# Layer 0's weighted sums with the features stationary, two heads on the two column halves of the array, turned back through DRAM

## The chip, the core and the metric

The program runs on one core of one Trainium2 chip. The metric is the device time in microseconds of one execution. Two runs of the kernel before gave 2604.69 and 2605.58 us, with a median of 2605.14 us. TensorE is written PE here, its weight load PEld, VectorE DVE, ScalarE ACT, GpSimd POOL, and the engine whose queue issues the DMAs SP.

## The reference, cut to what matters

The input is 128 graphs of 128 nodes with 256 features, `x` (128, 128, 256), and one adjacency matrix for each graph, `adj` (128, 128, 128), with entries 0 and 1. Four layers follow each other, each with a residual sum and a layer norm: attention with 4 heads of 64 features (layer 0), three steps of a gated recurrent unit (layer 1), a relational sum (layer 2), attention with one head (layer 3). The change is in layer 0:

```python
Wh = (X @ W).reshape(B, N, H, F)                  # H = 4 heads, F = 64 features
e = leaky_relu(e_src[:, :, None, :] + e_dst[:, None, :, :], 0.2)
alpha = softmax(where(A > 0, e, NEG_INF), axis=2)
Hout = einsum('bijh,bjhf->bihf', alpha, Wh)       # the weighted sums
x = layernorm(x + elu(Hout))
```

All data are 32-bit floats.

## The kernel before, in words

The graphs are worked in 33 groups: one of 2, then 31 of 4, then one of 2. A group passes through stages, each written as a generator: `l` loads, `h` layer 0 (`head`), `u` and `v` the elementwise work of the recurrent unit for the two halves of the features (`chunk`), `p` and `q` its matrix products (`gates`, two gates each), `t` layers 2 and 3 (`tail`). The order of all work is written out by hand as strings: each letter advances one stage of one group to its next `yield`. `START` (with the letters of `FIRST`) fills the pipeline, `STEPS` (`PERIOD`) is one period and is run 29 times, `END` (`LAST`) drains it. The instructions of each engine run in exactly the order in which the strings emit them; that holds for the DMAs on SP too. A period advances stages of up to seven groups (offsets 2 to -4).

In `head`, the scores of two graphs (`em`, 128 x 1024: 2 graphs x 4 heads x 128 columns) go through the softmax without its division. A first turn through DRAM follows: `to_dram` writes `em`, `from_dram` reads it back as 32 x 32 squares into `aT` (four DMAs), and DVE transposes within the squares (line 550). Only for group 0 (`by_pe`) does PE turn it. Then each head's `aT` is the stationary operand and that head's 64 columns of `wh` are the moving one: 8 matrix products of 64 columns for two graphs (line 132, called in `head`), into one bank `ps` of PSUM with nodes on the partitions. DVE multiplies the bank by the reciprocal denominators `den` straight into `x1` (line 558). Such a set of 8 products is called a block below; there are 64 of them (two for each group of 4, one for each group of 2), 63 with `by_pe` off.

`em` and `aT` share a ring of three buffers. The banks of PSUM are rings of three (`ps`), three (`sums`) and three (`gate`) by tag. `bank` adds products of zeros (`still`, 512 columns) ahead of the banks that `WARM` lists, 22 of them in the program.

In `gates` a product of two block matrices is done with seven instead of eight partial products, so that partial results have to be moved between halves of two banks: after the first products, ACT copies the half `c21` of `gate` into the half `c11` of `sums` (line 638) and `c22` aside into `p5` (line 640), DVE adds `c12 = c21 + p5` (line 648), and later `c22 = c21 + p5` (line 656). After each of these, PE adds further products into the same banks, so each is a hand-over from PE to another engine and back to PE. In `neighbours`, ACT copies a bank into `agT` (line 611), which PE then takes as a moving operand: another hand-over. The order strings set how much other PE work lies inside each hand-over.

A turn through DRAM in `turn_rows` and `chunk` is the same pair of DMAs with a DVE transpose behind it; SP issues the read only after the write has landed.

Of the kernel before, what the change touches and what calls it, by code (L numbers as in the profile page):

```python
# [9 lines left out]
F32 = mybir.dt.float32  # L10
# [3 lines left out]
ALU = mybir.AluOpType  # L14
AX = mybir.AxisListType

P = 128
N = 128
D = 256
C = D // P  # L20
H, F = 4, 64
# [2 lines left out]
Q = 32  # L24
G = 4
GATES, OTHERS = 3, 2
WARM = {0: 1, 5: 4, 16: 1, 23: 1, 24: 1, 1555: 1, 1557: 5, 1558: 1, 1563: 4, 1568: 3}
BY_PE = {"head": (0,), "rows0": (0, 1, 2), "gru1": (0, 1, -1, -2), "gru2": (0, 1, -1, -2), "rows3": (-1,), "tail": (-1, -2)}
EPS = 1e-5
SLOPE = 0.2  # L30
# [21 lines left out]

FIRST = {"a": ("f", 0), "b": ("c", 0), "c": ("h", 0), "d": ("l", 1), "e": ("h", 1), "f": ("l", 2), "g": ("u", 0), "h": ("q", 0), "i": ("v", 0), "j": ("p", 0), "k": ("h", 2), "l": ("l", 0), "m": ("l", 3), "n": ("u", 1), "o": ("q", 1), "p": ("v", 1), "q": ("p", 1), "r": ("h", 3), "s": ("t", 0)}
START = """
abbbbcccacaccacaccaccccacaccbcacaaaacadcccdcacccaaccbcccccececcceeccebeceecceeceecefccceecefecacccca
cgghegbhiiihehijjhghejaaeieeihhjeejjejjajjadhjehjbjjeijjeajaiakhgghjhjhehijhelajhakgejahhghjeagghaaj
khhgieiggggeheiggihjgejiihgeeeekkiehjliijkjeijeeehiihjkeikhjjhhjkjeeijkjekjhjiejhjkkaikhajkjkjkhgaak
hghhaejhehhhgaikjmheknnghanjogjiognhpaqqqgmpqiopigqqphpoqqqghikrkpqooqgqgniokqoigkoqoaqpkpoqioqoiion  # L60
goqqkpoqggoqqojkikolqqkjoppnniijjpokjhiokjhnnkjhniljojfjhnhojhpjjhjgnrnphhnkjpjinjhipjjiknhkhhjkggjj
hjonhgnkjihrpkkhpkkkkpohkqoqikhrhqgqpkhgqhgqokphqgkroqhpqkrpiqirqkoqirnsqoboqorpkrqqokrqqpqsroopsooq
nqrknorqrqnnorsssooo
"""
PERIOD = {"a": ("t", -3), "b": ("p", -1), "c": ("q", -1), "d": ("t", -2), "e": ("u", -1), "f": ("v", -1), "g": ("h", 0), "h": ("l", 2), "i": ("u", 0), "j": ("q", 0), "k": ("p", 0), "l": ("v", 0), "m": ("h", 1), "n": ("t", -4), "o": ("l", 1), "p": ("l", -1), "q": ("h", 2), "r": ("t", -1)}
STEPS = """
abcdefghdiiccjifkeafdjdkdljckeeicdddfdkmmknloldjkljlkedkfjmkmlejfjknamkfdmmamkfkdjeikjikldkldekkdjed
dlaikjjdjdkbemkdfdkbkjbfnbmjbkajffjjbjfpmblbmbibjjlajcfchbdjccqlimicdcbilddmidbddcqlcimeddmabdbnbccd
fibmlfmaqfbbamlibcceeccmbbdceeclccbcibciddcfcmidfedecidemcjmqfklmjnklfkqqkjmmqmlkjfjmkmllmmkdkkqkjdr
mmdrlmkkjmdqkqmjikqjjqkqrlkdkkkljrjmikljjkjdkrjqiqikijjjqr  # L70
"""
LAST = {"a": ("l", -1), "b": ("t", -4), "c": ("p", -3), "d": ("q", -3), "e": ("h", -2), "f": ("v", -3), "g": ("u", -2), "h": ("t", -5), "i": ("u", -3), "j": ("q", -2), "k": ("v", -2), "l": ("p", -2), "m": ("h", -1), "n": ("t", -6), "o": ("t", -2), "p": ("t", -1), "q": ("l", -3), "r": ("t", -3), "s": ("u", -1), "t": ("v", -1), "u": ("p", -1), "v": ("q", -1), "w": ("l", -2)}
END = """
abcdbefbgghggdiidhjkfbdljbdllbbjikllbkjbmbbjilkmkfklljmfmhniljbimlihhjjnflmlbgllkfjmfbkolblkmimjbmlm
ihfjgllfnjcblcbjbimlcmljmjbjlfjmjbflnggjpchcjfkfjmgcghbcddbcmmjfckkhdcdbjcgcmgiddcgbbbdgdckmdfkmdbob
fcfbcimbcbkdccdbddjcckiiddbmbccdqgkmddkcmmgibmdfmfddiikbgmdljgimdbfflgkljlklfjjbmlbkllkhjljlnrllmljl
mhjjkblkrlkjmlmmjjjlggbjrllrgbjjrjllbjrblrbjlmmkrstjusbjrsrrvugvgjgkvukrsghgrgrrujvkuttrrtuktgtukvuu
rukkrbuvrvubrurgvsgvrusruuukvtuugukuktrtuvsrlvugslrgvsvlkrvsrhvulvtwvlkjlvjjlbvvllvjltjlsvvjklrjjjsg
rtbsrthjlrtrlrhkkrrlrbsbspkljjllrlbrgjbtslsltsbvgjjlgsgrtlvttjljjjtkujurtrkjguvgurbkujtvrvujvuugujku
vtkusuuvououvovtoutruvrovsvvvuruuvvorvvuurvtaosusooouvstrtovvosvotosrsotsrtostrotsvrsvoovuststousovu  # L80
tvbtuvtvvutrouvuuuuovoovotovuuouutrooroootsoourrsouvvuovuuvvvuusovsbuuvstusvvtsvvstttotpopoopoppboro
poooppoppprprpprpopppoppooppoppopppporpppopporppppopoppppppppppppoppopoopppppppppp
"""


# [5 lines left out]
def kernel(ctx: ExitStack, tc: tile.TileContext, a: dict, out: bass.AP):  # L91
    nc = tc.nc
# [4 lines left out]
    NG = len(sizes)  # L97
    spans = [slice(sum(sizes[:i]), sum(sizes[: i + 1])) for i in range(NG)]

    cp = ctx.enter_context(tc.tile_pool(name="const", bufs=1))  # L100
    sp = ctx.enter_context(tc.tile_pool(name="work", bufs=1))
# [6 lines left out]
    def ring(pool, shape, dtype, tag, name, bufs):  # L108

        k = taken[tag] = (taken.get(tag, -1) + 1) % bufs  # L110
        return pool.tile(shape, dtype, tag=f"{tag}_{k}", name=name, bufs=1)
# [4 lines left out]
    def bank(*shape, tag="ps"):  # L116

        t = ring(pp, [P, 512], F32, tag, tag, OTHERS if tag == "ps" else GATES)
        banks["taken"] = banks.get("taken", -1) + 1
        for _ in range(WARM.get(banks["taken"], 0)):  # L120
            nc.tensor.matmul(t, still[:, :P], still, start=True, stop=True)
        n = 1
        for s in shape:
            n *= s
        if len(shape) == 1:
            return t[:, :n]
        names = "abcd"[: len(shape)]
        sizes = {k: s for k, s in zip(names[1:], shape[1:])}
        return t[:, :n].rearrange(f"p ({' '.join(names)}) -> p {' '.join(names)}", **sizes)

    def matmul(ps, lhsT, rhs, start=True, stop=True):
        nc.tensor.matmul(ps, lhsT, rhs, start=start, stop=stop)  # L132
# [10 lines left out]
    nc.gpsimd.memset(negbig, NEG)  # L143

    spread = cp.tile([P, NG], F32, tag="spread", name="spread")

    def squares(t, src):

# [151 lines left out]
    def to_dram(name, *parts):  # L300

        d = ring(dp, [sum(part.shape[1] for part in parts) * P, P], F32, "turn", f"d_{name}", 8)
        lo = 0
        for part in parts:
            hi = lo + part.shape[1] * P
            nc.sync.dma_start(d[lo:hi].rearrange("(k p) m -> p k m", p=P), part)
            lo = hi
        return d

    def from_dram(t, d):  # L310

        squares(t, d)
        return t
# [140 lines left out]
    def head(st):  # L454

        g0, n, by_pe = st["g"], st["n"], st["by_pe"]["head"]
        if by_pe:
            xT = sp.tile([P, C, n * N], F32, tag="x0s", name=f"x0s_{g0}")
            for c in range(C):
                ps = bank(n, N)  # L460
# [3 lines left out]
        else:  # L464
            xT = st["x0s"]
            flat = xT.rearrange("p c m -> p (c m)")
# [9 lines left out]
        for g in range(G):  # L476
            if g < n:
                ps = bank(D + 2 * H)
# [48 lines left out]
        for k in range(0, G, 2):  # L527
# [2 lines left out]
                if not by_pe:  # L530
                    from_dram(aTs[k].rearrange("p g h n -> p (g h n)"), ems[k])
            yield
        y = ring(sp, [P, n, D], F32, "x1", f"x1_{g0}", 3)
        nc.vector.reciprocal(den, den)
        yield
        for k in range(0, G, 2):
            if k >= n:
                for _ in range(3):
                    yield
                continue  # L540
            aT = aTs[k]
            if by_pe:
                for j in range(2):
                    ps = bank(H, N)
                    for h in range(H):
                        transpose(ps[:, h, :], ems[k][:, j, h, :])
                    nc.vector.tensor_copy(aT[:, j], ps)
            else:
                flat = aT.rearrange("p g h n -> p (g h n)")
                nc.vector.transpose(flat, flat)  # L550
            yield
            cols = slice(k * H, (k + 2) * H)
            ps = bank(2, H, F)
            for j in range(2):
                for h in range(H):
                    matmul(ps[:, j, h, :], aT[:, j, h, :], wh[:, k + j, ts(h, F)])
            yield
            nc.vector.tensor_tensor(
                y[:, k : k + 2, :].rearrange("p g (h f) -> p (g h) f", h=H),
                ps.rearrange("p g h f -> p (g h) f"),  # L560
                den[:, cols].unsqueeze(2).to_broadcast([P, 2 * H, F]),
                ALU.mult,
            )
            yield
        yield from residual_elu_norm(y, "x0", st, "x1", "0")
        st["edge"] = ring(sp, [P, n, N], F32, "edge", f"edge_{g0}", 4)
# [169 lines left out]
    def tail(st):  # L736
# [31 lines left out]
        for k in range(0, G, 2):  # L768
            half(k)
            yield  # L770
        adj_T = st["adj_s"]
        step = n // relations

        def related(k):
            rel = sp.tile([P, step, relations, N], F32, tag="rel", name=f"rel_{g0}_{k}")
            rows = adj_T.rearrange("p (g n) -> p g n", g=n)[:, k : k + step, :]
            for r in range(relations):
                nc.vector.tensor_scalar(rel[:, :, r, :], rows, float(r + 1), None, ALU.is_equal)
            return rel
# [1 line left out]
        later = rest()  # L781
        next(later)
        if by_pe:
            nc.vector.transpose(adj_T, adj_T)
            rel = related(0)
        yield
        yield from later
        x2 = st["x2"]
        if not by_pe:
            nc.vector.transpose(adj_T, adj_T)  # L790
            rel = related(0)
        y = ring(sp, [P, n, D], F32, "x3", f"x3_{g0}", 2)
        half, rest = layernorm(y, st, "x3")
# [141 lines left out]
            last[i.engine] = i  # L935


    total = sp.tile([P, 1], F32, tag="total", name="total")
    nc.vector.tensor_reduce(total, spread, AX.X, ALU.add)
    ones = sp.tile([P, 1], F32, tag="ones", name="ones")  # L940
    nc.vector.memset(ones, 1.0)
    ps = bank(1)
# [58 lines left out]
```

## Time and profile before

| | |
|---|---|
| median of 2 runs | 2605.14 us |
| the profiled execution | 2605.27 us |
| its span, first to last instruction | 2603.5 us |
| busy share of the span: PE, PEld, DVE, ACT, POOL | 99%, 87%, 82%, 73%, 32% |
| mean granted PE clock | 0.996 of full |
| DMA | 353.75 MB in 1,495,113 packets, 136 GB/s |
| DMA share of its 16 engines, between 400 and 2300 us | 0.76 to 0.77 |
| blocks of layer 0 (line 132, 128x64) | 1024 records, 273 ns mean |

One 32-bit matrix product appears as two records on PE, one for each of two passes, and as two weight loads on PEld; a transpose by PE has one record of each. A record of a product lasts longer than the distance to the next, since products are pipelined: what a product costs is the distance from its start to the start of the next. In a line of the timeline, the columns are the start in us, the length in us, engine, line, operation, output and input tiles, shape, and the number of instructions merged into the line; in brackets stands the idle time ahead and what ended it. In a line of the table by stretch, the columns are the stretch, its length, the busy time of PE, PEld, DVE, ACT and POOL with the number of instructions, the granted clock, the DMA share and GB/s.

### The profile page before, as it was taken

How to read it: one execution, taken by the hardware profiler on the slowest of the kernel's cores; microseconds unless marked ns; L12 is line 12 of the kernel's file. 1: busy time of each engine (PE TensorE's matmuls, PEld its weight loads, DVE VectorE, ACT ScalarE, POOL GpSimd, SP SyncE). 2: the span in 40 equal slices, each digit the busy share in tenths (PEclk: the TensorE clock that was granted, in tenths of full speed). 3: DMA queues.
4: the chain of work that ended last, by engine and by line, in shares of the span. 5: the costliest groups of instructions: out<-in, count | busy, mean ns of one | idle time of the engine just before them, and what ended most of it. 6: DMA issues, size and time to landing. Idle time of an engine off the chain costs nothing. (4 is left out here: it accounts for less than half of the span.)

```text
span 2603.5 us, 43906 instructions
## 1 busy us (share of the span) xinstructions
PE 2568.5 (99%) x13488; PEld 2263.5 (87%) x13488; DVE 2137.3 (82%) x4570; ACT 1899.3 (73%) x5099; POOL 841.4 (32%) x923
## 2 busy tenths in 40 slices
PE   8999999999999999999999999999999999999997
PEld 5888888888888888888888888888888888888885
DVE  5778888888888888888888888888888888887775
ACT  5666777777777777777777777777777777776666
POOL 0233423333322333323333323333322333332332
PEclk9999999999999999999999999999999999999999
DMA  5456777876777777777787777787778787777431
GB/s 124 75 107 126 139 145 145 151 150 141 148 143 150 148 150 140 151 138 152 146 152 147 140 148 147 148 148 150 139 147 153 145 153 145 140 141 135 92 58 36
DMA packets 1495113, 353.75 MB, mean 136 GB/s; under 512 B 1176280, under 2 KB 1479512, under 8 KB 1494872
## 3 DMA queue, kind: packets, MB, share of 16 engines
q1 hardware_dynamic: 1494872, 350.87, 69.8%
q8 instruction: 111, 1.82, 0.3%
q14 instruction: 130, 1.06, 0.1%
HBM read 213.00 MB, written 137.72 MB: 135 GB/s over the span
## 5 line engine op out<-in xcount | busy, mean ns | idle before, releaser
L628 PE MATMUL gate<-T_a,factors 128*128 128x256 f32 (+1 forms) x2376 | 686.0, 373 | 0.4 <-DVE gate L656 0.4
L628 PE MATMUL gate<-T_h,factors_h 128*128 128x256 f32 (+1 forms) x2376 | 676.1, 375 | 3.6 <-DVE gate L656 3.2
L628 PEld LDWEIGHTS gate<-T_h,factors_h 128*128 128x128 f32 x2376 | 438.0, 190 | 68.5 <-DVE gate L656 11.7
L628 PEld LDWEIGHTS gate<-T_a,factors 128*128 128x128 f32 x2376 | 443.1, 190 | 57.4 <-DVE gate L656 0.6
L628 PE MATMUL sums<-agT,factors 128*128 128x256 f32 (+1 forms) x1188 | 348.3, 375 | 1.0 <-ACT sums L638 0.7
L638 ACT COPY sums<-gate 128x256 f32<-128x256 f32 (+1 forms) x396 | 140.5, 355 | 201.1 <-PE gate L628 197.4
L353 POOL TENSOR_TENSOR rs_x<-rs_x,neghalf 128x4 f32<-128x4 f32 (+1 forms) x99 | 98.7, 997 | 537.4 <-DVE rs_x L352 528.1
L397 ACT ACTIVATE em<-em,nm 128x128 f32<-128x128 f32 x640 | 248.1, 391 | 28.5 <-DVE nm L394 26.2
L360 ACT ACTIVATE x<-x,mr_x,rs_x 128x256 f32<-128x256 f32 x384 | 199.6, 594 | 88.9 <-DVE mr_x L355 88.8
L628 PEld LDWEIGHTS sums<-agT,factors 128*128 128x128 f32 x1188 | 218.3, 190 | 28.9 <-ACT sums L638 1.9
L695 POOL TENSOR_TENSOR d<-h0T,n 128x512 f32<-128x512 f32 (+1 forms) x66 | 83.1, 1260 | 402.3 <-ACT n L692 402.2
L132 PE MATMUL ps<-wh,aT 128*128 128x64 f32 (+1 forms) x1280 | 188.8, 294 | 4.2 <-ACT n L686 3.0
L132 PEld LDWEIGHTS ps<-wh,aT 128*128 128x128 f32 x1280 | 170.0, 191 | 18.8 <-ACT gate L680 4.6
L611 ACT COPY agT<-ps 128x512 f32<-128x512 f32 (+1 forms) x198 | 113.4, 572 | 88.8 <-PE ps L132 88.3
L680 ACT ACTIVATE gate<-gate,bhalf 128x512 f32<-128x512 f32 (+1 forms) x198 | 127.9, 646 | 66.4 <-PE gate L628 66.2
L628 PE MATMUL gate<-agT,factors 128*128 128x256 f32 (+1 forms) x594 | 173.0, 373 | 0.0
L507 ACT ACTIVATE own<-nbias,wh 128x128 f32<-128x128 f32 x512 | 162.2, 396 | 0.0
L692 ACT ACTIVATE n<-n,bih 128x512 f32<-128x512 f32 (+1 forms) x198 | 140.3, 710 | 18.9 <-DVE n L690 18.8
L347 DVE BATCH_NORM_STATS2 st_x<-x 128x6 f32<-128x256 f32 x384 | 139.9, 413 | 0.1
L132 PE MATMUL ps<-w,x0s 128*128 128x264 f32 x512 | 134.8, 387 | 0.2 <-ACT wh L483 0.2
L680 ACT ACTIVATE sums<-sums,bhalf 128x512 f32<-128x512 f32 (+1 forms) x198 | 126.2, 637 | 11.9 <-PE sums L628 11.9
L765 POOL TENSOR_TENSOR x<-x,x 128x512 f32<-128x512 f32 x61 | 76.3, 1271 | 174.0 <-DVE x L762 170.8
(180 smaller groups left out, 5900.3 us busy)
## 6 DMA issues: line engine op xcount, KB each, us to landing
em<-d_rows SPq DMA_DIRECT2D x149, 256.0 KB
d_em<-em SPq DMA_DIRECT2D x63, 512.0 KB
aT<-d_em SPq DMA_DIRECT2D x252, 128.0 KB
x0s<-in_x_dram SPq DMA_DIRECT2D x248, 64.0 KB
x<-in_x_dram SPq DMA_DIRECT2D x31, 512.0 KB
d_h0T<-x SPq DMA_DIRECT2D x62, 256.0 KB
h0T<-d_h0T SPq DMA_DIRECT2D x124, 128.0 KB
out_dram<-o SPq DMA_DIRECT2D x31, 512.0 KB
```

The costliest lines, as they stand in the source:

```text
L132: nc.tensor.matmul(ps, lhsT, rhs, start=start, stop=stop)
L347: nc.vector.bn_stats(sums[:, g, :], y[:, g, :])
L353: nc.gpsimd.tensor_tensor(rs, rs, neghalf[:, :n], ALU.pow)
L360: nc.scalar.activation(y[:, g, :], y[:, g, :], AF.Identity, bias=mr[:, g : g + 1], scale=rs[:, g : g + 1])
L397: nc.scalar.activation(em[:, r, :], em[:, r, :], AF.Exp, bias=nm[:, i : i + 1], accum_out=den[:, i : i + 1])
L507: nc.scalar.activation(own[:, g - k, h, :], nbias[:, g, :], AF.Identity, bias=wh[:, g, D + h : D + h + 1])
L611: nc.scalar.copy(t, ps)
L628: nc.tensor.matmul(into, w[:, SEL[name], k - 1], layer[source][k], start=start, stop=True, skip_group_check=True)
L638: nc.scalar.copy(c11, c21)
L680: nc.scalar.activation(t, t, AF.Tanh, bias=bhalf[:, col : col + 1], scale=0.5)
L692: nc.scalar.activation(n, n, AF.Tanh, bias=bih[:, 2 * C + c : 2 * C + c + 1])
L695: nc.gpsimd.tensor_sub(d, hT, n)
```

## The change

For every group but the first, the operands of the 8 products are exchanged: one head's 64 columns of `wh` are stationary, `aT` of that head is moving with 128 columns, and the result has features on the partitions. Two heads are put on the two column halves of the array: the outputs go to partitions 0 to 63 and 64 to 127 of the same bank. The built program carries a tile size of 128 x 64 and tile positions (0, 0) and (0, 64) in turn for them. The result has to be turned back to nodes on the partitions: ACT copies the bank (128 x 512) into the first half of `aT`, SP writes it to DRAM and reads it back as squares into the same place (one DMA and four), DVE transposes it into `x1`, and DVE multiplies `x1` by `den` in place. All order strings are new. `WARM` keeps one of its entries, for bank 0. The reduction of `total` moves from the end of the program into the last group's `tail`, and `adj_T` is no longer bound early.

```diff
-WARM = {0: 1, 5: 4, 16: 1, 23: 1, 24: 1, 1555: 1, 1557: 5, 1558: 1, 1563: 4, 1568: 3}
+WARM = {0: 1}
...
-FIRST = {"a": ("f", 0), "b": ("c", 0), "c": ("h", 0), ...
+FIRST = {"a": ("h", 0), "b": ("c", 0), "c": ("f", 0), ...
...
(START, PERIOD, STEPS, LAST, END: all new)
...
-        y = ring(sp, [P, n, D], F32, "x1", f"x1_{g0}", 3)
         nc.vector.reciprocal(den, den)
+        turned = {}
         yield
...
                 nc.vector.transpose(flat, flat)
             yield
-            cols = slice(k * H, (k + 2) * H)
-            ps = bank(2, H, F)
-            for j in range(2):
-                for h in range(H):
-                    matmul(ps[:, j, h, :], aT[:, j, h, :], wh[:, k + j, ts(h, F)])
-            yield
-            nc.vector.tensor_tensor(
-                y[:, k : k + 2, :].rearrange("p g (h f) -> p (g h) f", h=H),
-                ps.rearrange("p g h f -> p (g h) f"),
-                den[:, cols].unsqueeze(2).to_broadcast([P, 2 * H, F]),
-                ALU.mult,
-            )
+            if by_pe:
+                ps = turned[k] = bank(2, H, F)
...
+            else:
+                ps = bank(2, C, N)
+                for j in range(2):
+                    for c in range(C):
+                        for i in range(2):
+                            matmul(ps[ts(i, F), j, c, :], wh[:, k + j, ts(2 * c + i, F)], aT[:, j, 2 * c + i, :])
+                yield
+                yT = aT.rearrange("p g h n -> p (g h) n")[:, : 2 * C]
+                nc.scalar.copy(yT, ps.rearrange("p g c n -> p (g c) n"))
+                turned[k] = yT.rearrange("p c n -> p (c n)")
+                from_dram(turned[k], to_dram(f"y_{g0}_{k}", yT))
+            yield
+        y = ring(sp, [P, n, D], F32, "x1", f"x1_{g0}", 3)
+        for k in range(0, G, 2):
+            if k < n:
+                flat = y[:, k : k + 2, :].rearrange("p g d -> p (g d)")
+                scaled, raw = (t.rearrange("p (b f) -> p b f", f=F) for t in (flat, flat))
+                if by_pe:
+                    raw = turned[k].rearrange("p g h f -> p (g h) f")
+                else:
+                    nc.vector.transpose(flat, turned[k])
+                cols = slice(k * H, (k + 2) * H)
+                nc.vector.tensor_tensor(scaled, raw, den[:, cols].unsqueeze(2).to_broadcast([P, 2 * H, F]), ALU.mult)
             yield
...
+        if g0 == NG - 1:
+            nc.vector.tensor_reduce(total, spread, AX.X, ALU.add)
...
-    total = sp.tile([P, 1], F32, tag="total", name="total")
-    nc.vector.tensor_reduce(total, spread, AX.X, ALU.add)
```

## The prediction

> **What bounds the kernel.** I read the page's first part first, then the table by stretch.
>
> ```profile
> PE 2568.5 (99%) x13488; PEld 2263.5 (87%) x13488; DVE 2137.3 (82%) x4570; ACT 1899.3 (73%) x5099; POOL 841.4 (32%) x923
> ...
> 1200.00:1600.00 400.00, 400.00 (x2086) 356.02 (x2085) 341.02 (x717) 299.51 (x797) 133.17 (x144) 1.00 0.77 147
> ```
>
> In the middle PE is busy 400.00 of 400 us at full clock, DVE 85%, ACT 75%, DMA 77%. A busy PE is not proof of a full one, so I laid the starts of all products against the shape's own pace (256 columns 0.432 us for the two passes, 128 columns 0.222, 264 columns 0.446): between 400 and 2200 us only 5.9 us are lost. PE's work is the time there. A period (one group) lasts 77.55 us: a block starts at 1361.97 and its successor one group later at 1439.52. The chain that ended last holds only the final layer norm and tells nothing of this.
>
> Next, what a block costs: the timeline of PE around one.
>
> ```profile
> 1361.54 0.59 PE L628 MATMUL gate<-T_h,factors_h 128*128 128x256 f32 x2
> 1361.97 1.94 PE L132 MATMUL ps<-wh,aT 128*128 128x64 f32 x16
> 1363.75 0.65 PE L628 MATMUL sums<-agT,factors 128*128 128x256 f32 x2
> 1364.24 0.59 PE L628 MATMUL gate<-T_a,factors 128*128 128x256 f32 x2
> ```
>
> 16 records from 1361.97 to 1363.75 are 1.78 us, 0.111 each, as much as a record of 128 columns (0.222/2): the 64 columns bring nothing. The product behind takes 0.49 instead of 0.43. So 1.84 us; the group's other block (1372.04 to 1373.77) gives 1.79. I take 1.82.
>
> **The packing: -45 us.** After, 16 records of 128 moving columns stand in two column halves in turn. If the halves run beside each other, 16 records take 8 slots of 0.111 and one more to fill: 1.00 us. If not, 1.78. No block of column halves is in the trace. The nearest row for a change of the array's shape is the 16-row block:
>
> ```profile
> 107.31 0.59 PE L628 MATMUL gate<-agT,factors 128*128 128x256 f32 x2
> 107.84 2.05 PE L132 MATMUL ps<-rows,ident 16*128 16x128 f32 x16
> 109.81 0.70 PE L628 MATMUL gate<-h0T,factors_h 128*128 128x256 f32 x2
> 110.35 0.38 PE L628 MATMUL gate<-T_a,factors 128*128 128x256 f32 x1
> ```
>
> It starts 0.10 late (107.74 was due), its 16 records take 1.97 instead of 1.78, and the product behind takes 0.54 instead of 0.43: 0.21 at the borders, 0.19 within. A one-pass product with a stationary tile of 128x16 (at 83.72, its neighbours at 83.50 and 83.83) shows no border at all. So a block lies between 0.89 (halves perfectly beside each other) and 2.18 (one after the other, with the 16-row block's losses). I take 1.00 plus half the borders, 1.10, since the only column tile in the trace is free and the row tile is not. Saved: 0.72 x 63 blocks = 45 us; ends: 59 saved, 23 lost.
>
> The Trainium skill ("TensorEngine Tiling (Array Packing)", Key Properties) speaks against the change here: a change of the tiling mode drains the engine. It gives no figure; the trace agrees for the rows' tile (0.21) and not for the one column tile. Drained like the rows, each block would cost 1.21 and the packing save 38 us.
>
> **New orders: the hand-overs, +76 us.** This term is not in the change's words. I went through the built programs in PE's order and, for each product that waits for another engine's result of an earlier product, summed the PE work between the two by the paces above. Before, no hand-over between 400 and 2200 us has under 0.86 us of PE work inside, and all 163 of 0.86 to 0.89 cost nothing. After, every period has six that are shorter or longer-running: ACT's copy `c21` to `c11` (line 638, after 656) with 0.00 inside, DVE's `c12` (648, after 666) twice with 0.43, DVE's `c22` (656, after 674) once with 0.43, ACT's `agT` (611, after 629) with 0.43, and a `gate` bank taken again with 0.86 inside while ACT's 128x512 read of it (686, after 704) takes 0.70; before, that distance was 2.18 at least. PE runs in order, so nothing behind such a product can fill the wait. The fill and drain of before have the same hand-overs and price them. First 0.00 through ACT, then 0.43 through DVE:
>
> ```profile
> 224.12 0.59 PE L628 MATMUL gate<-T_a,factors 128*128 128x256 f32 x2
> 224.75 0.39 ACT L638 COPY sums<-gate 128x256 f32<-128x256 f32 x1
> 225.20 0.70 PE L628 MATMUL sums<-agT,factors 128*128 128x256 f32 x2 [0.48 <-ACT sums L638]
> 225.73 0.59 PE L628 MATMUL gate<-T_a,factors 128*128 128x256 f32 x2
> ...
> 2473.17 0.43 DVE L656 TENSOR_TENSOR gate<-gate,p_r 128x256 f32<-128x256 f32 x1 [2.03 <-PE gate L628]
> 2473.75 0.67 PE L628 MATMUL gate<-T_h,factors_h 128*128 128x256 f32 x2 [0.18 <-DVE mv_o L351]
> 2474.26 0.59 PE L628 MATMUL gate<-T_a,factors 128*128 128x256 f32 x2
> ```
>
> The first was due at 224.55 and starts at 225.20, and the next is 0.53 behind it: 0.65 + 0.10 = 0.75 lost. The second was due at 2473.40: 0.35 + 0.08 = 0.43; another (four records from 2470.46, the next at 2471.68, 1.22 instead of 0.87) lost 0.35, so 0.39 in the mean. Through ACT with 0.43 inside, one at 149.88 lost 0.28; `agT`'s copy is 0.59 instead of 0.36 long, so 0.51. The bank: 0.75, plus 0.70 - 0.39 for the longer read, less 0.86, is 0.20. A period: 0.75 + 3 x 0.39 + 0.51 + 0.20 = 2.63 us, x 29 = 76 us. Bounds: half of it, if the copy at 224.75 was late for ACT's own sake and the bank's wait is none (38), and a fifth more, if the engine is still at something else when the hand-over arrives (91).
>
> **The turn back: +15 us.** Two turns a period. On ACT one copy of 128x512 (0.59, row of line 611) twice: 58.1 + 1.2 of 77.55 us, hidden beside PE. On DVE one transpose (0.70, `h2N`, line 726) twice: 66.1 + 1.4, hidden; the scaling out of the bank (0.68) becomes one in place (0.69). On DMA 0.5 MB a block, 33 MB in all to 353.75: the share goes from 0.77 to about 0.84 by bytes. None is the bound. But SP issues the read right behind the write, and so stands until the write has landed:
>
> ```profile
> 1402.54 0.39 SPq L711 DMA_DIRECT2D d_h<-h2T  x1
> 1404.97 1.92 SPq L151 DMA_DIRECT2D h2N<-d_h  x4
> ...
> 1036.60 3.02 SPq L151 DMA_DIRECT2D x3T<-d_x3T  x4
> 1043.89 1.25 DVE L333 STREAM_TRANSPOSE x3T<-x3T 128x1024 f32<-128x1024 f32 x1 [0.48 <-DMA x3T<-d_x3T]
> ```
>
> Write to read is 2.43 us, the four issues 1.92, and of a read of twice the size the last landed 4.27 after its issue (1039.62 to 1043.89). With 0.2 to start ACT's copy and 0.59 for it, a turn takes 7.1 (landing 2 us after the issue, as a write does) to 9.4 us. In the new order PE has 10.05 us of work between the first block's end and two products that need DVE's additions (674 and 666), and DVE has to do the transpose, the scaling and both additions back to back ahead of them: 0.6 + 0.6 + 0.35 + 0.43, with 0.15 to PE. That leaves about 8: from 0.9 to spare to 1.4 late. I take 0.5 late a period, the value in the middle, 15 us. Bounds: 0, and 2.5 us (72 us) if SP reaches the write late, since the four reads of `h1N` (2.09 us) and a write of `d_rows`, which waits for DVE, are queued ahead of it. Behind the standing SP wait `d_h`, `em3` and the second turn; their results are used over 9 us after their writes, and the second turn has 13 us.
>
> **Fill and drain: -5 us.** 21 warm-up products of 0.86 us go, 18 us of PE work, most of it where PE lost 22 (first 100 us) and 11 us (last 200) anyway; the new strings have some dozen more short hand-overs there of about 0.3. Bounds -15 and +15. `total` leaves the end, but its reduction was done before the last graphs were: 0.
>
> **Sum.** The profiled execution took 2605.27 us (span 2603.5), 0.13 above the median. -45 + 76 + 15 - 5 = +41: 2646 us, 1.6% slower.
>
> **Rivals.** *Hand-overs are hidden* (the other side): the copy needs only `c21`, whose last product lies one product earlier than I counted, and engines with spare time (DVE 14%, ACT 24%) answer sooner. It decides from the point where a period's hand-overs cost under (45 + 5 - 15)/29 = 1.2 us instead of 2.63; at none the time is 2646 - 76 = 2570. For it: 163 short ones were free. Against: all those had 0.86 inside, and the rows at 224 and 2473 are the same lines with less. *The halves don't run beside each other*: blocks of 1.78 to 2.18 instead of 1.10, +43 to +68: 2689 to 2714. For it: the 16-row block gained nothing; against: nothing in the trace makes the second half wait. *The turn comes late*: the upper bound of that term, +57: 2703, seen as DVE waiting for the DMA of `aT` ahead of the new transpose.
>
> **How the numbers follow.** My forecast 0.52 (own range 2615 to 2675; a quarter of it above 2657), hidden hand-overs 0.16, no overlap 0.17, late turn 0.15. A measurement here is told from no change at about 2%: 2553 to 2657. Slower by over 2%: 0.13 + 0.17 + 0.15 = 0.45; faster by over 2%, hidden hand-overs with the best packing (2556) and a shorter drain: 0.04; within: 0.51. The range 2570 to 2705 leaves out the lower half of the second case and the upper part of the third, some 0.16.
>
> **What would show it.** Right: a period of about 79 us; block starts to the next product 1.1 us; PE no longer at 400 of 400 but some 12 us short in 400, the idle time in front of lines 646 put down to ACT 656, ACT 629, DVE 666 and 674. Wrong: PE as full as before, blocks at 1.8, or DVE idle over 1 us a period in front of the new transpose (579).

## The result and the profile after

The changed kernel takes 2687.14 us (median of 2 runs, 2683.39 to 2690.90) against 2605.14 us before: a ratio of 1.0308, with a 95% interval of 1.0292 to 1.0324, so 3.1% slower. The prediction of 2646 us had half of that loss: 41 us were expected and 80 to 82 came. The time lies inside the range of 2570 to 2705, but outside the forecast's own 2615 to 2675. Of the four terms of the sum, the hand-overs met their size, the packing was a little high, the turn back came near its size for a wrong reason, and fill and drain were far off.

The profiled execution took 2690.90 us (span 2688.7). The table by stretch (columns as before: stretch, length, busy time of PE, PEld, DVE, ACT, POOL, granted clock, DMA share, GB/s):

```profile
0.00:100.00 100.00, 77.34 (x377) 55.88 (x378) 54.24 (x124) 47.40 (x157) 7.43 (x20) 0.88 0.46 109
1200.00:1600.00 400.00, 393.05 (x2026) 331.89 (x2025) 338.91 (x708) 297.67 (x790) 131.83 (x141) 1.00 0.76 156
```

PE is no longer full in the middle (393.05 of 400, before 400.00), nor is any other engine the bound in its place: VectorE stands at 85%, ScalarE at 74%, the DMA engines at 76%. In the first 100 us PE is busy for 77.34, where it was 89.25 before, and the clock granted there is 0.88 instead of 0.97. In the timelines, one block of layer 0 and one hand-over with nothing inside:

```profile
1412.85 0.59 PE L646 MATMUL gate<-T_a,factors 128*128 128x256 f32 x2
1413.55 1.09 PE L132 MATMUL ps<-aT,wh 128*64 128x128 f32 x16
1414.57 0.70 PE L646 MATMUL sums<-h2T,factors_h 128*128 128x256 f32 x2
...
1045.25 0.59 PE L646 MATMUL gate<-T_a,factors 128*128 128x256 f32 x2
1045.88 0.36 ACT L656 COPY sums<-gate 128x256 f32<-128x256 f32 x1 [0.20 <-PE gate L646]
1046.29 0.70 PE L646 MATMUL sums<-agT,factors 128*128 128x256 f32 x2 [0.45 <-ACT sums L656]
1046.83 0.59 PE L646 MATMUL gate<-T_a,factors 128*128 128x256 f32 x2
```

The 16 records of a block now take 1.02 us from their start to the next product's start (1413.55 to 1414.57), against 1.78 before: two halves of 64 columns do run beside each other. In the hand-over, the product that needs ACT's copy was due at 1045.68 (1045.25 plus 0.43) and starts at 1046.29, and the one behind it comes 0.54 later instead of 0.43. So 0.72 us are lost, where the prediction had 0.75.

The most frequent period is 79.59 us (11 of 27; the mean is 79.96), before 77.54. To see where the 85 us between the two profiled spans went, I cut each span at the first input product of layer 0 (`ps<-w,x0s`) of group 5 and of group 32, the same 27 periods of work:

| us | to group 5 | 27 periods | rest | span |
|---|---|---|---|---|
| before | 288.4 | 2100.9 | 214.2 | 2603.5 |
| after | 311.9 | 2159.0 | 217.8 | 2688.7 |
| difference | +23.5 | +58.1 | +3.6 | +85.2 |

Over a quarter of the loss is in the fill, which the prediction had put down as a gain.

### The profile page after: what moved, and what is told of

It reads as the page before. It is cut to its first block, busy times and chain, and to the rows that moved or that the text cites. A ratio compares the mean times of both kernels' runs of the same rounds, so it can differ in the third digit from the quotient of the medians.

```text
span 2688.7 us, 44591 instructions
## 1 busy us (share of the span) xinstructions
PE 2589.1 (96%) x13446; PEld 2178.1 (81%) x13446; DVE 2185.0 (81%) x4633; ACT 1934.0 (72%) x5162; POOL 841.8 (31%) x923
## 5 line engine op out<-in xcount | busy, mean ns | idle before, releaser
L646 PE MATMUL sums<-agT,factors 128*128 128x256 f32 (+1 forms) x1188 | 356.4, 382 | 21.9 <-ACT sums L656 14.6
L609 POOL TENSOR_TENSOR T_h<-h1T,T_h 128x256 f32<-128x256 f32 (+1 forms) x66 | 47.8, 724 | 325.0 <-PE gate L646 319.8
L713 POOL TENSOR_TENSOR d<-h1T,n 128x512 f32<-128x512 f32 (+1 forms) x66 | 90.2, 1367 | 179.4 <-ACT n L710 179.4
L646 PE MATMUL sums<-h1T,factors_h 128*128 128x256 f32 (+1 forms) x396 | 120.6, 387 | 10.4 <-ACT sums L656 5.5
```

What stands on the lines that cost most here:

```text
L646: nc.tensor.matmul(into, w[:, SEL[name], k - 1], layer[source][k], start=start, stop=True, skip_group_check=True)
L713: nc.gpsimd.tensor_sub(d, hT, n)
```

## The experiments

Each time is a median; the ratio in brackets is to the kernel before on the same chip, with its 95% interval. Microseconds "by ratio" are the ratio times 2605.14. Spans and periods are those of the profiled executions.

### The two parts apart: packing alone, orders alone

The kernel before with the packed block in its own orders and nothing turned back:

```diff
+            if by_pe:
                 ps = bank(2, H, F)
...
+            else:
+                ps = bank(2, C, N)
+                for j in range(2):
+                    for c in range(C):
+                        for i in range(2):
+                            matmul(ps[ts(i, F), j, c, :], wh[:, k + j, ts(2 * c + i, F)], aT[:, j, 2 * c + i, :])
```

> The kernel before, its orders and warm-ups kept, with the packing alone: the blocks that take their weights from the DMA turn become products of 128 moving columns in two column halves, and VectorE scales straight out of the bank as before. The turn back is left out, so layer 0's weighted sums stand in the wrong layout; all else is computed as before. Theory (the packing works, with border losses like the row tile's): a block of 1.21 us in place of 1.82, 63 blocks, 38 us saved: 2567 us. Rival (a block gains nothing, or what it gains turns into waits for VectorE, which scales at once): 2605 us. If the packing is as cheap as I forecast (1.10 us): 2560 us.

It took 2576.16 us (0.9883, 0.9866 to 0.9899): 30 us by ratio, not 38. The most frequent period is 76.37 us, 1.17 shorter than before. By the trace, the rest of the 38 went into a wait that the kernel before has once, for 0.2 us; PE's waits between 400 and 2300 us (engine, line, waited for: us in total, times, longest us) hold

```profile
PE gate L637 <- DVE gate L665: 8.1, 8, 2.2
```

The other way round, the new orders with the old block (the ACT copy kept, its view rearranged, neither DMAs nor transpose):

```diff
-                ps = bank(2, C, N)
+                ps = bank(2, H, F)
...
-                from_dram(turned[k], to_dram(f"y_{g0}_{k}", yT))
...
-                    nc.vector.transpose(flat, turned[k])
+                    raw = turned[k].rearrange("p (b f) -> p b f", f=F)
```

> The changed kernel with the old block of 64 moving columns in it: the new orders, ScalarE's copy of the bank and VectorE's scaling are kept, the turn through DRAM and VectorE's transpose are left out (the layout is right without them). Theory (the new orders cost what was lost, the packing gives 38 us back, the turn is hidden): 2687 + 38 = 2725 us, period about 81.2 us. Rival (the turn is what costs; without it the new orders are as good as the old): 2650 us or less.

It took 2701.76 us (1.0372, 1.0355 to 1.0390), 97 us by ratio. The orders, with ACT's copy in them, cost more than the whole change does. The 27 periods last 2173.5 us, 72.6 more than before: 2.69 us a period, where the prediction had 2.63. The fill takes 310.0 us (+21.6), the rest 215.1 (+0.9).

### Hand-overs alone, in the kernel before

If the hand-overs are the cause, they must cost the same without anything else of the change. Here three letters of `STEPS` of before move by a few places, so that one ACT copy `c21` to `c11` has nothing inside and another has 0.43 us, and a product that takes a `gate` bank again comes one product sooner after ACT's read of that bank (686); nothing else differs:

```diff
-fibmlfmaqfbbamlibcceeccmbbdceeclccbcibciddcfcmidfedecidemcjmqfklmjnklfkqqkjmmqmlkjfjmkmllmmkdkkqkjdr
-mmdrlmkkjmdqkqmjikqjjqkqrlkdkkkljrjmikljjkjdkrjqiqikijjjqr
+fibmlfmaqfbbamlibcceecbcmbdceeclccbcibciddcfcmidfedecidemcjmqfklmjnklfkqqkjmmqmlkjfjmkmllmmkdkkqkjdr
+mmdrlmkkjmdqkqmjikqjjqkqrlkdkkjklrjmikljkjjdjkrqiqikijjjqr
```

> The kernel before with three letters of its period's string moved, so that in each of the 29 periods three products of TensorE stand nearer to the ScalarE copy c21 to c11 that they wait for: one directly behind the product that the copy reads (0.00 us of work inside), two with one product of 0.43 us inside; 0.86 us in the kernel before. Nothing else is changed. Theory (a short hand-over is paid in full, at the prices of the prediction: 0.75 and twice 0.28 us): 1.31 x 29 = 38 us, 2643 us, period 78.85. Rival (a hand-over is hidden by engines with spare time): 2605 us, period 77.55.

It took 2647.80 us (1.0148, 1.0131 to 1.0165): 39 us by ratio, as the theory said. In its timeline:

```profile
1417.92 0.59 PE L628 MATMUL gate<-T_a,factors 128*128 128x256 f32 x2
1418.61 0.36 ACT L638 COPY sums<-gate 128x256 f32<-128x256 f32 x1 [2.42 <-PE gate L628]
...
1419.02 0.70 PE L628 MATMUL sums<-h1T,factors_h 128*128 128x256 f32 x2 [0.50 <-ACT sums L638]
...
1419.55 0.59 PE L628 MATMUL gate<-T_a,factors 128*128 128x256 f32 x2
```

ACT had been idle for 2.42 us when PE handed over, so its copy wasn't late for its own sake; still 0.67 us pass (due 1418.35, start 1419.02), and 0.10 behind it. The copy reads `c21` alone, whose last product starts at 1417.06 and whose record ends at 1417.65; yet it starts only 0.10 after the record of the last product into `c22` ends (1418.51), so here it waits for that one too. The copy with 0.43 inside lost 0.28 (0.18 ahead, 0.10 behind), the 0.28 of the expectation. The third product does not wait for a copy, as the expectation has it: at 1177.52 it starts 0.06 after ACT's read of the bank (686) ends, and it lost 0.30. The three are 1.35 us together; the period is 78.90 us, 1.36 more than before, and three letters moved in a string of 358 are worth 1.5% of the time.

### The turn back: none, and with its transpose alone

The changed kernel without the DMAs and with the transpose left out too, and then without the DMAs only:

```diff
 (both)
-                from_dram(turned[k], to_dram(f"y_{g0}_{k}", yT))
...
 (the first only)
-                    nc.vector.transpose(flat, turned[k])
+                    raw = turned[k].rearrange("p (b f) -> p b f", f=F)
```

> The changed kernel without the turn back: no write to DRAM, no read, no transpose on VectorE; the packed products, ScalarE's copy and the scaling (from the copy) stay, so layer 0's weighted sums stand in the wrong layout. Theory (the turn is never waited for in the middle, and its work lies beside TensorE): 0 to 8 us faster than the changed kernel, 2679 to 2687. Rival (the turn's queue time, DMA traffic or VectorE's extra 1.4 us a period make the short hand-overs late): 30 to 45 us faster, 2642 to 2657.

> The changed kernel without the turn's DMAs (no write of d_y, no read back), but with VectorE's transpose of the copy and the scaling in place kept; layer 0's weighted sums stand in a wrong layout. Without both, 2663.0 us were measured, 24 us less than the changed kernel. Theory (the transpose, 0.70 us more on VectorE ahead of the scaling, makes ScalarE's ELU wait, and ScalarE's copies of wh behind it free the bank late): as slow as the changed kernel or nearly, 2678 to 2687, with the wait of the first-layer products for ScalarE's copy of wh of about 0.5 us a period still there. Rival (the turn's DMAs, SP's standing or DMA traffic are what cost the 24 us): 2663 to 2668, with that wait gone.

Without any turn it took 2662.98 us (1.0220, 1.0203 to 1.0237), between the two expectations; with the transpose alone 2688.00 us (1.0303, 1.0286 to 1.0320), as the whole change takes (1.0308). So the DMAs cost 1 us by ratio, which isn't told from nothing, and VectorE's transpose 22 us. The prediction had it the other way round: the transpose hidden, the wait for the DMAs 15 us.

How a hidden transpose costs PE time is seen in the timelines around the scaling. First the changed kernel, then the one without a turn:

```profile
1033.43 0.70 DVE L579 STREAM_TRANSPOSE x<-aT 128x512 f32<-128x512 f32 x1
1034.17 0.69 DVE L581 TENSOR_TENSOR x<-x,den 128x512 f32<-128x512 f32 x1
1034.89 0.63 ACT L377 ACTIVATE elu<-x 128x512 f32<-128x512 f32 x1 [0.73 <-DVE x L581]
1035.43 0.36 ACT L484 COPY wh<-ps 128x264 f32<-128x264 f32 x1
1035.84 1.16 PE L132 MATMUL ps<-w,x0s 128*128 128x264 f32 x4 [0.25 <-ACT wh L484]
```

```profile
1025.84 0.68 DVE L580 TENSOR_TENSOR x<-aT,den 128x512 f32<-128x512 f32 x1
1026.56 0.63 ACT L377 ACTIVATE elu<-x 128x512 f32<-128x512 f32 x1
1026.95 1.94 PE L132 MATMUL ps<-w,x0s 128*128 128x264 f32 x8
1027.10 0.36 ACT L484 COPY wh<-ps 128x264 f32<-128x264 f32 x1
```

VectorE is the only engine that does more, and it has idle time elsewhere. But the 0.70 us stand directly in front of the scaling. ACT's first step of the ELU (377) waits 0.73 us for the scaling, ACT's copy of a PSUM bank of `wh` (484) is queued behind it, and PE needs that bank for the next input product. Without the transpose, none of them waits here, and PE runs eight records on end. The waits between 400 and 2200 us, ACT's in the changed kernel first, then ACT's and PE's with the transpose but no DMAs:

```profile
ACT elu L377 <- DVE x L581: 16.4, 22, 1.0
```

```profile
ACT elu L377 <- DVE x L580: 16.1, 22, 0.7
...
PE ps L132 <- ACT wh L484: 5.5, 22, 0.3
```

PE's in the changed kernel is 5.8 us, 22 times (shown further below). Each comes about once a period, with and without the DMAs; without a turn neither is in the list. With the starts laid against their paces, this input product is 0.41 us late and the next one 0.10: 0.5 of the 0.70 us a period that the transpose costs (2157.9 less 2139.1 us over the 27 periods). The rest lies in smaller delays that were not followed. The transfer itself was in time: between 400 and 2200 us the transpose waits for the DMA of `aT` once, for 0.2 us.

The packing is read between two runs that share the new orders, the old block and the packed one, neither turned: 1.0372 less 1.0220 is 40 us, and in the 27 periods 2173.5 less 2139.1, or 1.27 us a period and 0.64 a block. A block of the run without a turn:

```profile
1402.10 0.59 PE L645 MATMUL gate<-T_a,factors 128*128 128x256 f32 x2
1402.63 1.09 PE L132 MATMUL ps<-aT,wh 128*64 128x128 f32 x16
1403.65 0.70 PE L645 MATMUL sums<-h2T,factors_h 128*128 128x256 f32 x2
1404.19 1.03 PE L645 MATMUL gate<-T_h,factors_h 128*128 128x256 f32 x4
```

It starts 0.10 late (due 1402.53), takes 1.02, and the product behind it takes 0.54 instead of 0.43: 1.23 in all, with the whole 0.21 at the borders that the 16-row block of before has.

### The fill: its order, and the warm-up products

The kernel of the new orders with the old block loses 21.6 us before group 5. To part the order from the rest, it got the `START` of before, each old step of the block's scaling made into the new steps, and the seven warm-up products of that fill, so two things change at once; all periods and the drain stay the new ones:

```diff
-WARM = {0: 1}
+WARM = {0: 1, 5: 4, 16: 1, 23: 1, 24: 1}
...
 START = """
-aaabbbbccaaacacccaccbaacaacccabcaccaaa...
+cbbbbaaacacaacacaacaaaacacaabacaccccac...
```

> The new orders with the old block (ACT copy kept, no turn), as in the run that put the orders alone at 2701.8 us, but with the fill in the order of the kernel before: its START letter for letter, each old step of the block's scaling made into the new steps (copy; then, behind the second copy, both scalings), four letters that reach further than the new START left off, one added, and the five warm-up entries of the fill back. From the first period on, all is the new orders. Theory (the order of the fill itself costs what the fill lost): the first input product of group 5 comes at 286 to 292 us instead of 310.0 (before: 288.4), and the time is 2678 to 2686, ratio 1.028 to 1.031. Rival (the fill is longer because the blocks' new steps, ACT's copy in front of the scaling, stand in it, whatever the order): 304 us or later, and 2695 to 2703, ratio 1.034 to 1.038.

It took 2689.83 us (1.0323, 1.0306 to 1.0341), between the two again and nearer the theory: the old `START` with its warm-up products is worth 13 us by ratio, and group 5 begins at 295.8 us instead of 310.0. The table's first stretch, for the new `START` (old block) and for the old one:

```profile
0.00:100.00 100.00, 82.47 (x394) 61.56 (x395) 54.09 (x122) 50.13 (x165) 8.69 (x20) 0.86 0.43 104
```

```profile
0.00:100.00 100.00, 88.60 (x488) 66.93 (x489) 61.60 (x138) 57.70 (x197) 12.71 (x26) 0.98 0.46 109
```

With the starts of all products laid against their paces, PE loses 38.2 us in the first 100 us with the new `START`, 20.8 with the old one and 22.2 in the kernel before; the old one does 6 us more of warm-up products. Of the remaining 7 us before group 5, about 5 are the new periods' own hand-overs: the periods begin near 160 us, and from 160 to 300 us PE loses 8.5 us instead of 3.7. So of the 21.6 us, 14 are the new `START` and its missing warm-up products, 5 belong to the hand-overs, and the rest is as small as the cut is rough: that input product stands a little later in the new period.

What that order loses in the changed kernel, PE's waits of the first 100 us show, and the chain behind the longest of them:

```profile
PE sums L646 <- ACT sums L656: 6.2, 2, 5.0
PE ps L132 <- ACT w1T L285: 3.0, 1, 3.0
PE ps L132 <- DVE aT L551: 2.3, 1, 2.3
```

```profile
88.43 0.71 DVE L579 STREAM_TRANSPOSE x<-aT 128x512 f32<-128x512 f32 x1 [4.28 <-DMA aT<-d_y]
...
89.91 0.63 ACT L377 ACTIVATE elu<-x 128x512 f32<-128x512 f32 x1 [4.52 <-DVE x L581]
...
91.62 0.28 ACT L656 COPY sums<-gate 128x128 f32<-128x128 f32 x1
...
91.96 0.79 PE L646 MATMUL sums<-h1T,factors_h 128*128 128x128 f32 x2 [4.99 <-ACT sums L656]
```

This is the late turn of the prediction's third rival: here, with little other work to lie beside it, VectorE waits 4.28 us for the turned sums, ACT behind VectorE, ACT's copy of a hand-over (656) behind the ELU in its queue, and PE behind that copy. It happens in the fill alone, and the time shows little of it: the changed kernel's fill is only 0.3 us longer than that of the run without a turn (311.6).

The warm-up products, which the prediction took for free work removed, were tried in both directions: taken out of the kernel before, and put into the changed kernel (26 of them, at banks of its own fill and drain).

```diff
 (kernel before)
-WARM = {0: 1, 5: 4, 16: 1, 23: 1, 24: 1, 1555: 1, 1557: 5, 1558: 1, 1563: 4, 1568: 3}
+WARM = {0: 1}
...
 (changed kernel)
-WARM = {0: 1}
+WARM = {0: 1, 5: 2, 20: 2, 33: 1, 47: 3, 49: 2, 57: 5, 1481: 1, 1556: 3, 1563: 4, 1568: 3}
```

> The kernel before with only the first of its warm-up entries kept (the entry of the changed kernel): 20 warm-up products fewer, 17 us less work for TensorE at full clock. Theory (removing them is what left the clock at half speed for about 24 us of the changed kernel's fill and more of its drain): 10 to 20 us slower, 2615 to 2625, with granted clock under 0.95 in the first 100 us. Rival (the products filled idle time and cost or gave nothing, as I forecast): 2590 to 2605 us.

> The changed kernel with 26 warm-up products put back, ahead of the banks where its fill and drain stood idle for over 1 us and the granted clock then fell to half (16 in the fill, 10 in the drain). Taking them out of the kernel before cost it 10.5 us. Theory (the missing warm-ups are part of the loss in fill and drain): 8 to 20 us faster than the changed kernel, 2667 to 2679, and less time at half clock. Rival (the clock falls because of the waits themselves, and the products add work): 2685 to 2700.

The first stretch of each, the kernel before without them and the changed kernel with them:

```profile
0.00:100.00 100.00, 84.24 (x441) 65.11 (x442) 57.72 (x130) 52.59 (x180) 8.13 (x21) 0.90 0.50 102
```

```profile
0.00:100.00 100.00, 84.34 (x408) 57.25 (x409) 54.39 (x124) 47.70 (x157) 7.45 (x20) 0.96 0.47 110
```

Out of the kernel before (21 of its 22; the expectation counts 20), they cost it 9 us (2616.04 us; 1.0034, 1.0020 to 1.0048): the clock granted in the first 100 us falls from 0.97 to 0.90. Group 5 begins 4.9 us later there (293.3 us instead of 288.4), so up to 5 of the 14 us that the old `START` brought can be its warm-up products; no run has that order without them. Put into the changed kernel, they raise it from 0.88 to 0.96 and change nothing (2687.46 us; 1.0303, 1.0286 to 1.0320). A higher clock is worth nothing there; the waits shown above suggest why, as the longest of that fill are for other engines, but no run tried it.

### Can the packing be had without the new orders?

Two kernels tried it. The first has the packing and the whole turn for groups 3 to 31 (the others keep the old block), in orders made from those of before, with the write, the read and the transpose of a turn as steps of their own that are spread apart. In its orders one addition on VectorE (`tensor_add(n, n, ni)`) is issued ahead of that bank's last product, so a part of that sum is left out.

```diff
+        def write(k):
+            if packed and k in turned:
+                back[k] = to_dram(f"y_{g0}_{k}", turned[k].rearrange("p (c n) -> p c n", n=N))
+
+        def read(k):
+            if k in back:
+                from_dram(turned[k], back[k])
```

> The packed block with its turn, put into orders that keep the old ones' hand-overs: TensorE's products stand as in the kernel before but for the second block of a group, which is moved some 5 us ahead; the turn's write and read back are steps of their own, so that SP does not stand between them; VectorE's and ScalarE's steps of layer 0 are moved so that none of their results comes late; groups 0 to 2 and the last keep the old block; the warm-ups are the old ones. Theory (what the changed kernel lost, it lost to its orders and to VectorE's transpose standing in the wrong place; neither is bound to the packing): 29 to 30 of 33 groups gain up to 1.24 us each, less what is left of waits, period 76.4 to 76.9 against 77.55: 2580 to 2590 us. Rival (the transpose and the turn cost the packed block its gain wherever they stand, as 24 of the 39 us in the changed kernel): 2605 to 2620 us.

It took 2654.68 us (1.0184, 1.0169 to 1.0199), worse than either expectation. The second keeps the order of PE's products of the kernel before to the letter and packs and turns only the first of the two blocks of a group (groups 3 to 31):

```diff
+        packed = not by_pe and st["g"] in range(3, NG - 1)
...
+        turn(0)
+        yield
+        if not packed:
+            old_products(0)
...
+        else:
+            ps = bank(2, C, N)
...
+            back[0] = to_dram(f"y_{g0}", yT)
```

> The kernel before, its products in the old order, with only the first of a group's two blocks packed and turned back (groups 3 to 31); the second keeps 64 columns and is scaled out of its bank. The turn has the time between the two blocks, about 10 us: its write and its read back are steps of their own, some 2.4 us apart, and VectorE's transpose and scaling stand where the scaling of the second block stood. The result is the reference's. Theory (the packed block keeps its 0.61 us where no result of the new work comes late and no hand-over is shortened): 29 x 0.61 = 18 us less at most, some of it lost to landings that come late: 2588 to 2598 us. Rival (the transpose, 0.70 us of VectorE a group, is paid by TensorE wherever it stands, as in the changed kernel, 25 us for two of them): 2600 to 2612 us.

It took 2651.79 us (1.0187, 1.0173 to 1.0201), again worse than either. Its waits between 400 and 2200 us and its timeline show where; the queue of SP is among the lines (SPq):

```profile
DVE em L907 <- DMA em<-d_rows: 30.1, 20, 2.3
...
PE gate L668 <- DVE gate L696: 25.5, 44, 1.5
```

```profile
1231.48 0.44 SPq L307 DMA_DIRECT2D d_y<-aT  x1
1232.02 0.45 SPq L429 DMA_DIRECT2D em<-d_rows  x1
...
1237.90 0.69 DVE L907 TENSOR_TENSOR em<-em,nbias 128x512 f32<-128x512 f32 x1 [1.97 <-DMA em<-d_rows]
...
1240.76 0.42 DVE L696 TENSOR_TENSOR gate<-gate,p_z 128x256 f32<-128x256 f32 x1
1241.09 0.70 DVE L563 STREAM_TRANSPOSE x<-aT 128x512 f32<-128x512 f32 x1
...
1241.23 0.70 PE L668 MATMUL gate<-T_h,factors_h 128*128 128x256 f32 x2 [1.06 <-DVE gate L696]
```

The read of `em` for layer 3 now stands behind the write of the turn on SP. It lands 5.9 us after its issue (1232.02 to 1237.90), much as in the kernel before (5.8, from 1209.98 to 1215.74, where it was waited for). But it is issued 2.4 us later in the period (69.0 us behind the group's first input product instead of 66.6, medians), and VectorE is ready for it only 0.5 us later; the write takes 0.54 of the 2.4, the rest was not followed. VectorE waits 1.97 us for it, then has its work back to back up to a hand-over of `gates` (696), and PE waits 1.06 us. Before, the same wait for `em<-d_rows` adds up to 1.9 us in that stretch, here to 30.1. The first kernel has the like ahead of its transpose between 400 and 2200 us, and PE waits once a period for an addition of `gates` (710):

```profile
PE gate L682 <- DVE gate L710: 36.4, 23, 2.3
...
DVE x L588 <- DMA aT<-d_y: 29.2, 40, 1.9
```

That these waits are the cause in the two kernels is read from their traces and was not tried by itself. What the runs do show is that neither set of orders paid for the turn with the packing. No version tried with the turn in it beat the kernel before; that none can is not shown.

## Why the prediction was right or wrong

| term | predicted | measured | from |
|---|---|---|---|
| packing | -45 | -40 | orders alone against the change without a turn |
| hand-overs | +76 | +77 | 27 periods of the orders alone (72.6), and 5 us of the fill |
| turn back | +15 | +23 | 22 by the transpose, 1 by the DMAs |
| fill and drain | -5 | +20 | what is left of the 97 us of the orders |
| sum | +41 | +80 | |

The range held by luck: it reached to 2705 only for two rivals, halves one after the other (2689 to 2714) and a late turn (2703), and neither is what happened. Of the 39 us by which the sum is short, 25 are fill and drain, 8 the turn back, 5 the packing.

**The bound.** Right: in the kernel before, PE's work was the time in the middle, and time lost on PE appeared in full. Everything that follows rests on it, and three letters moved in a full PE queue cost the 39 us that the paces said.

**The packing.** Right in kind, 5 us too much. Wrong is the step "1.00 plus half the borders, 1.10": the slots took 1.02, but the borders came in full, for 1.23. The half was a mean of a row tile with borders and a column tile without; the latter was one lone product, a poor stand-in for a block. The rule of the Trainium skill ("TensorEngine Tiling (Array Packing)", Key Properties), that a change of the tiling mode drains the engine, agrees with these 0.21 us, and the 38 us that the prediction worked out beside it were nearer to the measured 40. In the orders of before the same blocks gave only 30, since PE, now faster, waited 8.1 us for one of VectorE's additions (665).

**The hand-overs.** The right mechanism at the right size, and the term was for the larger part the whole loss. PE's waits of the changed kernel between 400 and 2200 us name the lines that were predicted:

```profile
PE sums L646 <- ACT sums L656: 10.3, 23, 0.4
PE ps L132 <- ACT wh L484: 5.8, 22, 0.6
PE sums L646 <- ACT agT L629: 5.3, 22, 0.2
PE sums L646 <- DVE sums L666: 3.6, 22, 0.2
```

Such a wait is the time in which no record is open; the record ahead is 0.59 long at a pace of 0.43, so 0.16 more are lost, and 0.10 behind. With these, 0.45 + 0.26 = 0.71 for ACT's copy (0.75 predicted), 0.24 + 0.26 = 0.50 for `agT` (0.51) and 0.16 + 0.26 = 0.42 for one addition (0.39). The other three of the six leave no idle time and are read from the starts. One of them, the other addition `c12`, in the changed kernel:

```profile
1031.13 1.03 PE L646 MATMUL gate<-T_h,factors_h 128*128 128x256 f32 x4
...
1032.25 0.70 PE L646 MATMUL sums<-h1T,factors_h 128*128 128x256 f32 x2
...
1032.79 0.59 PE L646 MATMUL gate<-agT,factors 128*128 128x256 f32 x2
```

The waiting product was due at 1031.99 and starts 0.26 late, and 0.10 are lost behind it: 0.36. In the medians of the periods between 400 and 2200 us, the addition `c22` costs 0.36 too and the bank 0.23 (0.20 predicted). The six are 2.6 us together, against 2.63 predicted; what the orders alone lose beside them (2.69 us a period) lies in small waits that the prediction does not list. The prices are not constants: with 0.43 us inside, an addition cost 0.36 to 0.42 here, and a copy of ACT 0.28 in the kernel before. The sign "some 12 us short in 400" came as 7, since much of each loss lies inside open records, which count as busy. The line of `wh` is not a hand-over of the orders but the transpose's cost.

**The turn back.** The sum of +15 was not far from +23, by a step that was wrong and another that was left out. "I take 0.5 late a period" for SP, DMAs and VectorE is false: the DMAs cost 1 us, and between 400 and 2200 us the transpose waits for them once, for 0.2 us. The DMA share, forecast at 0.84, is 0.76: the turn does add 0.06 to 0.07, but the orders alone stand at 0.69 where the kernel before has 0.77 for the same bytes, which no run explains. "On DVE one transpose, ... hidden" is where it failed: I compared busy shares (66.1 + 1.4 of 77.55 us) and did not ask who stands behind the transpose. ACT does, and behind ACT's instruction the copy that frees a PSUM bank for PE. By my own rule for PE's queue I should have followed the edit one engine further.

**Fill and drain.** The largest miss, outside the term's own bounds of -15 and +15. The step "21 warm-up products ... go, 18 us of PE work, most of it where PE lost 22" with "some dozen more short hand-overs there of about 0.3" treats the new `START` as the old one with small changes. It is another order: PE loses 16 us more in the first 100 us even with the old block. About 14 us of the term are that order with its missing warm-up products (the run with the old `START`, which changes both; up to 5 of them can be the products); some 6 are left for the drain (0.9 us in the run of the orders alone, 3.6 in the changed kernel), for the joint of the strings and for the roughness of the cut, and stay open. That their removal is free work saved was wrong as well: the kernel before lost 9 us by it, and the changed kernel is no slower with 26 put back. A trace of before can't price a rewritten fill; I should have laid the new strings of the first 100 us against the durations of before, as I did for the periods, or kept a bound of more than 15 us.

**The rivals.** Hidden hand-overs are refuted (39 us by themselves in the kernel before, and the copy waits for the later product that it does not read); so are halves one after the other (1.02 us). The late turn, priced at 2703, is near the measured time by its number and not by its mechanism: it appears in the fill, and between 400 and 2200 us once, for 0.2 us.

## What to carry to other kernels

When an in-order engine is full, read every hand-over that a new order makes: with nothing inside it, a copy on another engine cost about 0.7 us, with 0.43 us of work inside 0.3 to 0.5, and with 0.86 nothing, or 0.2 where the other engine's instruction took 0.70. An instruction on an engine with spare time is hidden only if what is queued behind it, on its own engine and on those that wait for it, has time to spare as well. And a fill that is written anew is to be priced like a new kernel, not like the old one with less in it.

## What the hardware showed beside this

In the first of the last two kernels (packing and whole turn, orders made from those of before), VectorE and GpSimd get in each other's way. Its timeline:

```profile
1027.99 1.27 POOL L749 TENSOR_TENSOR d<-h1T,n 128x512 f32<-128x512 f32 x1 [2.79 <-ACT n L746]
1028.12 1.18 DVE L353 TENSOR_SCALAR rs_x<-mv_x 128x4 f32<-128x4 f32 x1
```

VectorE's instruction on 4 columns takes 1.18 us; its median over that stretch of the run is 0.17. It starts while a GpSimd instruction runs and ends 0.04 us after that (1029.26 and 1029.30). Over all the traces, `x<-x,den` (0.69 alone) took 1.14 us in the median and up to 1.68 when it started beside a running GpSimd instruction, and `x<-aT,den` (0.68) 1.23 and up to 1.28; the long ones end 0.55 after a GpSimd instruction does. Transposes and instructions that read PSUM kept their lengths beside GpSimd. The Trainium skill ("SBUF — State Buffer", the section on SBUF's two separate sides) describes a pair of ports that VectorE and GpSimd share, which one of them locks for a whole instruction; the rows agree with that. An order that moves a small VectorE instruction by a microsecond can so make it seven times as long.

A granted clock is no time by itself: the same kind of warm-up products raised it by 0.07 to 0.08 in both kernels' first 100 us and was worth 9 us in one and nothing in the other.
